# Attention and NF4 FFN on one core: wider scale loads, shifted pieces of the NF4 stream, and GpSimd taking the hidden-state splits

## The chip, the core and the metric

The kernel runs on one core of one Trainium2 chip. The core has TensorE (matmuls; the trace shows weight loads, PEld, apart from matmuls, PE), VectorE (DVE), ScalarE (ACT), GpSimd (POOL) and SyncE (SP), which issues nearly all transfers. Each engine works through its own list of instructions in order and waits on semaphores; 16 DMA engines move the data. The metric is the device time of one execution in microseconds. Before the change it was 789.08 us, the median of 3 runs (787.16 to 791.25).

## The reference

x is 8 batches of 128 rows of 512 floats, ctx the same shape. One cross-attention block with 32 query heads and 8 key/value heads of size 128, then a gated FFN whose three weights (hidden size 1376) are quantized to NF4 and back before they are used, all in float32.

```python
def nf4_quant_dequant(w):
    flat = w.reshape(-1, 64)
    absmax = jnp.max(jnp.abs(flat), axis=1, keepdims=True)
    normalized = flat / jnp.where(absmax == 0, 1.0, absmax)
    bounds = (NF4_CODE[:-1] + NF4_CODE[1:]) * 0.5
    idx = jnp.searchsorted(bounds, normalized)
    return (NF4_CODE[idx] * absmax).reshape(shape)
...
q = apply_rope(query @ Wq); k = apply_rope(key @ Wk); v = value @ Wv
logits = 30 * tanh(einsum(q, k) * 0.0883883 / 30)
weights = softmax(where(mask, logits, -1e30))
x = x + (weights @ v) @ Wo          # query is layernorm(x), key and value are ctx
h = silu(y @ dq1.T) * (y @ dq2.T)   # y is layernorm(x), dq1..dq3 went through NF4
x = x + h @ dq3.T
```

## The kernel before

**Matmuls.** Each float32 factor is split into a high and a low part (`split`, L154: ScalarE copies the high part in a rounded format, a second engine, named in the call, subtracts it from the source for the low part). `product` (L165) then makes three matmuls (high by low, high by high, low by high) for each pair of 128-row tiles, so that a 128x512 output over a depth of 512 takes 12 matmuls.

**Stages.** First the key and value projections and the first queries (0 to 124 us), written by a plan by tile number. Then 64 attention steps `i`, in 16 units `u` of four batches each: unit `u` belongs to key/value head `u // 2` and to the half `u % 2` of the batches, and step `i` to batch `bb = i % 4` of that unit. In one step TensorE makes: the query projection of head `bb` for the next unit (`pq`), the output projection of step i-3 (`po`), the transposes of step i-2 (`pt_a`), the values of step i-1 (`pv`), and the scores of step i (`pl`). After that comes the FFN's gate and up loop over 22 (half, hidden tile) pairs (`pg`, `pu`; to 724 us) and the down products (`pd`).

**The query's way.** VectorE multiplies `pq` by the cosine and sine tables into `cs_q` (L518); SP moves the two swapped halves, 64 rows each, into `full_q` (L521, L522); GpSimd adds (L525); `split` makes `qr` of it (ScalarE copy at L155, GpSimd subtraction at L156); the scores of the next unit read `qr`. In the steps with `bb == 3` the add stands ahead of the scores and the split behind them.

**The scores' way.** `pl` goes through tanh and exp on ScalarE (L815, L816), is multiplied by the mask on GpSimd (L818), and is the weights of `pv` in the next step.

**The NF4 stream.** `quantize` (a generator) works through 17 units of weights, 128 x 1024 each for most: `Up` units for w1 and w2 (ten of 256 columns and one of 2 x 128), and six `Down` units for w3. For each unit it loads the weights and the reciprocal scales, GpSimd normalises (L210), 15 bounds follow (a Relu on ScalarE at L200, an accumulation on VectorE at L204 or L206), and VectorE multiplies by the scales (`finish`). `store` splits the result. `pump(n)` runs n pieces of this stream, where a piece is about one bound, and the step's order fixes where the pieces stand among the other instructions of each engine. `Scales` units find absolute maxima between the bounds. `ask` queues the loads by rank; `serve`, twice a step, issues one of them, so that they stand on SP between the step's own loads.

**Scales.** The maxima of w1 and w2 are written to `scale_d` in DRAM and read back so that each value stands on the 64 partitions of its block (`Up.scale`, L264; `begin(1)` reads the reciprocals, `begin()` the maxima). Those of w3 go through `scale3_d`, written by eight stores (L369) and read by `Down.scale` (L226), each row repeated on 32 partitions.

**The FFN.** `load_w12` (L860) reads the finished w1/w2 tiles from DRAM, from the fourth tile on by GpSimd's own queue; each load waits until the matmuls have left one of six `wq` buffers. `split_h` (L1041) splits the hidden state into `hs`: four times in the last iterations of the gate and up loop, and then one or two for each down product.

Of the kernel before, what the change touches and what calls it, by code (L numbers as in the profile page):

```python
# [11 lines left out]
F32 = mybir.dt.float32  # L12
# [8 lines left out]
P = 128  # L21
B, T, D = 8, 128, 512
NH, NKV, HD = 32, 8, 128
G = NH // NKV
# [38 lines left out]
def block_kernel(ctx: ExitStack, tc: tile.TileContext, x, ctxt, mask, wq, wk, wv, wo, w1, w2, w3, w12t, w3_t,  # L63
# [151 lines left out]
    class Down(Unit):  # L215
# [10 lines left out]
        def scale(self, t):  # L226
            s = self.tile("nf_s", f"s{t}")
            for h in self.tiles:
                g = 1 + h * P // 32
                src = scale3_d[t, g:g + self.p // 32].rearrange("g e p -> g (e p)")  # L230
                for j in range(self.p // 32):
                    nc.sync.dma_start(self.part(s, h)[j * 32:(j + 1) * 32], src[j:j + 1].to_broadcast([32, D]))
            return s

        def load(self):
# [16 lines left out]
    class Up(Unit):  # L252
# [11 lines left out]
        def scale(self, t):  # L264
            s = self.tile("nf_s", f"s{t}")
            for j, part in self.parts(s):
                for half in range(2):
                    src = scale_d[self.start // (2 * P), t, j, half, :, :self.r]
                    nc.sync.dma_start(part[half * BLK:(half + 1) * BLK],
                                      src.unsqueeze(0).to_broadcast([BLK, KT, self.r]))  # L270
            return s

        def load(self):
# [57 lines left out]
    class Scales3:  # L331
# [23 lines left out]
        def turn(self, tag):  # L355
            pt = bank(tag, "pt_ar3").rearrange("b (t p) -> b t p", p=P)[:self.nb, :2]
            for t in range(2):
                E.transpose(pt[:, t], self.s[:, t], ident)

            def later():  # L360
                leave()
                art = nf.tile([self.nb, 2, P], F32, tag="nf_t", name="art3")
                S.copy(art, pt)
                half, stores = self.nb // 4 + 1, []
                for e in range(4):
                    first = (0, 21, 43, 64)[e]
                    g = 1 - e % 2
                    for t in range(2):
                        stores.append(lambda t=t, g=g, e=e, first=first: nc.sync.dma_start(  # L369
                            scale3_d[t, g:g + 2 * half, e].rearrange("(b g) p -> b g p", g=2),  # L370
                            art[first:first + half, t].unsqueeze(1).to_broadcast([half, 2, P])))
                for some in (stores[:4], stores[4:]):
                    ask(None, lambda some=some: [f() for f in some])
            stored.append(later)
# [95 lines left out]
    with ExitStack() as c1:  # L470
# [432 lines left out]
        for i in range(N):  # L903
            u, kv, b, bb = where(i)
            s8 = i % 8
            tiles = {0: (0, 1), 1: (2,), 2: (3,), 3: ()}.get(i, (bb,)) if u + 1 < 2 * NKV else ()

            turns = [q_proj(u + 1, g) for g in tiles]
            if i == 0:
                load_o(0, 0)  # L910
                todo["k", 0, 0]()
                adds.append(turns.pop(0)())
                load_o(0, 1)
                end_store()
                copied = ending[0]()
            if i != 2:
                adds += [f() for f in turns]
            if i == 0:
                load_o(0, 2)
                load_o(0, 3)  # L920
                ending[1]()
                copied()
            if kv + 1 < NKV:
                if s8 == 3:
                    load_kv(kv + 1)
                if 4 <= s8:
                    load_o(kv + 1, s8 - 4)
                elif kv:
                    load_q(kv + 1, s8)
                due.setdefault(max(i + 1, 2), []).append(("q" if s8 < 4 else "o", kv + 1, s8 % 4))  # L930
            if s8 == 0 and kv:
                load_key(kv, 1)
            if s8 == (0 if kv else 1):
                due.setdefault(i + 1 if kv else 3, []).append(("k", kv, 1))
            if s8 == 4 and kv + 1 < NKV:
                load_key(kv + 1, 0)
                due.setdefault(i + 1, []).append(("k", kv + 1, 0))
            if i == 1:
                V.tensor_tensor(lo, whole.pop(0)[2], hi, ALU.subtract)
            if i > 3:  # L940
                store()
                end_store()
            if i > 2:

                for _ in range(2):
                    serve()
            pump(2.3 if i == 4 else 2.15 if 4 < i < 58 else 2 if i == 58 else 0)
            if 0 <= i - 3:
                project(i - 3)
            if whole and i > 3:  # L950
                *own, full = whole.pop(0)
                split(*of_head(*own), full, Q)
            if i in (59, 61):
                ln = LayerNorm((i - 59, i - 58), f"y{i - 59}")
            if 0 <= i - 2:
                turn(i - 2)
            if i == 2:
                for _ in range(1, G):
                    todo[due[2].pop(0)]()
            if 59 <= i < 63:  # L960
                ln.sums(i - 59)
            if 0 <= i - 1:
                values(i - 1)
            if i == 2:
                adds += [f() for f in turns]
            if i == 0:
                end_store()
            if adds and i > 2 and bb == 3:
                whole.append((u + 1, bb, adds.pop(0)()))
            scores(i)  # L970
            if adds:
                whole.append((u + 1, bb, adds.pop(0)()))
            if i == 61:
                xn.update({k: pair.rows(k, "xn") for k in (0, 1)})
            if whole and i > 3 and bb == 3:
                *own, full = whole.pop(0)
                split(*of_head(*own), full, Q)
            pump(1 if 2 < i < 59 else 0)
            if i == 62:
                turned((0, 1), "qq")  # L980
            if i in (60, 62):
                ln.finish(Q)
                pair = ln
            normalize()
            leave()
            if i == 0:
                pump(1)
                hi, lo = of_head(1, 0)
                S.copy(hi, whole[0][2])
            while len(whole) > 3 - i and 1 < i < 4:  # L990
                *own, full = whole.pop(0)
                split(*of_head(*own), full, Q if i > 2 else V)
            if i == 2:
                pump(1)
            for k in due.pop(i, ()):
                todo[k]()
            if i == 1:
                load_q(1, 0)
                load_key(0, 1)
                load_q(1, 1)  # L1000
            if i == 2:
                load_q(1, 2)
                load_q(1, 3)
            if i >= 61:
                load_w12(i - 61)
# [35 lines left out]
    def split_h(b, i):  # L1041
        n = min(4, NHT - 4 * i)
        if (b, i) in last_hs:
            w = last_hs.index((b, i))
            if not last_at:
                last_at.append(wide("hs_67"))
            t = hs[b, i] = last_at[0][:, :, :, w * P:(w + 1) * P]
        else:
            t = hs[b, i] = wp.tile([P, 2, KT, P], F32R, tag="wq", name=f"hs_{b}_{i}", bufs=6)
        split(t[:, 0, :n], t[:, 1, :n], hT[b // 4, i][:, :, b % 4 * T:b % 4 * T + T], V)  # L1050

    order = [(0, 2), (1, 0), (1, 1), (1, 2)] + [(half, h) for h in range(3, NHT) for half in range(2)]
    most = [(b, i) for b in range(6) for i in range(2)]
# [5 lines left out]
    for n, (half, h) in enumerate(order):  # L1059
        evac()  # L1060
        evac = gate_up(half, h, f1)
        pump((3.6 if n < last - 3 else 2.6) if n > 0 else 0)
        store()
        if n in w12_at:
            load_w12(w12_at[n])
        if n >= last - 3:
            split_h(*to_split.pop(0))
    evac()
# [3 lines left out]
    for b, i in down:  # L1072
# [9 lines left out]
        if (b, i) in most:  # L1082
            if i == 1:
                product(pd[b], mine, stop=False)
                mine.clear()
            pump(2)
            store()
        elif i == 2:
            o = f1.tile([P, D], F32, tag="o", name=f"o_{b}", bufs=4)
            parts = 2 if b == B - 1 else 1  # L1090
            for j in range(parts):
                own = slice(j * D // parts, (j + 1) * D // parts)
                to = pd[b] if b < 6 else bank(("q", "q", "s")[b - 6 + j], f"pd_{b}_{j}")
                product(to[:, own], [(s, (th[:, own], tl[:, own])) for s, (th, tl) in mine], start=b >= 6)
                V.tensor_tensor(o[:, own], acc[b][:, own], to[:, own], ALU.add)
                nc.sync.dma_start(out[b][:, own], o[:, own])
# [36 lines left out]
```

## Time and profile before

| | us |
|---|---|
| median of 3 runs | 789.08 |
| profiled execution: its own time | 789.4 |
| profiled execution: span from first to last instruction | 787.6 |
| projections, 0 to 124: PE / DVE / ACT / POOL busy | 122.4 / 95.2 / 81.4 / 70.2 |
| attention, 124 to 568 | 436.2 / 391.4 / 340.8 / 358.2 |
| end of attention and gate/up, 568 to 724 | 153.2 / 130.6 / 102.1 / 46.2 |
| down products, 724 to 788 | 60.4 / 41.1 / 27.8 / 4.8 |

TensorE's granted clock is 1.00 of full in the first three stretches and 0.99 in the last. In the lines of a timeline the columns are: start, duration, engine, line, operation, out<-in, shapes, count of merged instructions, and in brackets the idle time just before it with what ended it. For SP the duration is that of issuing, not of the transfer; the landings stand in the semaphore records of the trace.

### The profile page before, as it was taken

What the parts mean: (1) busy time and instruction counts of PE and PEld (TensorE: products, weight loads), DVE (VectorE), ACT (ScalarE), POOL (GpSimd) and SP (SyncE); (2) the same over time, 40 slices, a digit from 0 to 9 for tenths busy, and PEclk for the clock granted to TensorE, in tenths of its full rate; (3) what the DMA queues carried; (4) which work ended last, traced back from release to release, by engine and by line L of the source; (5) the groups of instructions that cost most, each with busy time, mean ns of one, the idle gap of its engine ahead of it and who ended that gap; (6) DMA issues with size and microseconds to landing.
All of it is one profiled execution on the core that took longest, in us unless ns stands there. A gap on an engine that the chain in (4) does not pass through costs nothing.

```text
span 787.6 us, 11542 instructions
## 1 busy us (share of the span) xinstructions
PE 772.1 (98%) x3800; PEld 637.3 (81%) x3800; DVE 658.3 (84%) x863; ACT 552.1 (70%) x782; POOL 479.4 (61%) x418
## 2 busy tenths in 40 slices
PE   9999999999999999999999999999999999998998
PEld 7888887788878888888788877877888888886887
DVE  6768978979889889889789988798888697899981
ACT  7558657787886868687768868687642786779740
POOL 2569446787879789797888878887750222332100
PEclk9999999999999999999999999999999999999999
DMA  6966658637373837546473745463540334633011
GB/s 219 324 202 199 189 161 240 176 115 218 104 230 87 262 92 223 172 136 201 121 233 82 213 108 182 114 175 108 181 153 1 95 103 124 185 111 110 1 54 53
DMA packets 73219, 119.24 MB, mean 151 GB/s; under 512 B 9896, under 2 KB 31080, under 8 KB 73160
## 3 DMA queue, kind: packets, MB, share of 16 engines
q1 hardware_dynamic: 70856, 110.13, 47.0%
q0 software_dynamic: 2304, 8.39, 3.4%
q8 instruction: 30, 0.49, 0.3%
q14 instruction: 29, 0.24, 0.1%
HBM read 79.32 MB, written 22.38 MB: 129 GB/s over the span
## 4 chain that ended last, share of the span: by engine, by line
PE 65%; ACT 8%; POOL 7%; DVE 6%; DMA 6%; issue 5%; SPq 3%; POOLq 0%; DVEq 0%
PE po L170 15%; PE pq L170 13%; PE pd L170 8%; PE pvp L170 6%; ACT nm_w L200 5%; PE pv L825 5%; PE pl L170 4%; PE pk L170 3%; PE pg L170 3%; PE pu L170 3%; DVE nc_w L206 3%; DMA s_w<-scale_d 2%; PE pt_a L162 2%; PE pk L611 2%; DMA w_w<-in_w3t 2%
## 5 line engine op out<-in xcount | busy, mean ns | idle before, releaser
L206 DVE SCALAR_TENSOR_TENSOR nc_w<-nm_w,nc_w 128x1024 f32<-128x1024 bf16 (+1 forms) x238 | 284.0, 1193 | 48.9 <-ACT nm_w L200 38.6
L200 ACT ACTIVATE nm_w<-w_w,bias 128x1024 bf16<-128x1024 f32 (+1 forms) x255 | 276.2, 1116 | 45.7 <-POOL w_w L210 37.3
L170 PE MATMUL po<-wo,aT 128*128 128x512 f32 x768 | 192.7, 399 | 4.1 <-DVE acc L839 3.6
L170 PE MATMUL pq<-xT,wq 128*128 128x512 f32 x768 | 186.8, 392 | 1.9 <-DVE wq L156 1.2
L170 PEld LDWEIGHTS po<-wo,aT 128*128 128x128 f32 x768 | 141.5, 188 | 44.0 <-DVE aT L156 3.9
L170 PEld LDWEIGHTS pq<-xT,wq 128*128 128x128 f32 x768 | 143.4, 188 | 35.6 <-DVE cs_q L518 2.5
L818 POOL TENSOR_TENSOR th<-th,mt 128x512 f32<-128x512 f32 x64 | 83.6, 1306 | 60.8 <-ACT th L816 56.8
L525 POOL TENSOR_TENSOR full_q<-cs_q,full_q 128x512 f32<-128x512 f32 x64 | 83.4, 1303 | 21.0 <-DMA full_q<-cs_q 17.2
L156 POOL TENSOR_TENSOR qr<-full_q,qr 128x512 fp32r<-128x512 f32 x58 | 75.4, 1301 | 8.1 <-ACT qr L155 6.8
L518 DVE TENSOR_TENSOR cs_q<-pq,cq 128x1024 f32<-128x1024 f32 x64 | 77.6, 1214 | 0.9 <-POOL full_q L525 0.8
L825 PE MATMUL pv<-vt,th 128*128 128x129 f32 x512 | 68.2, 276 | 0.9 <-POOL th L818 0.9
L170 PE MATMUL pg<-xT,w 128*128 128x512 f32 x264 | 63.8, 391 | 2.8 <-ACT w3t L155 2.8
L815 ACT ACTIVATE th<-pl 128x512 f32<-128x512 f32 x64 | 38.3, 598 | 39.0 <-PE pl L170 38.7
L825 PEld LDWEIGHTS pv<-vt,th 128*128 128x128 f32 x512 | 62.2, 192 | 2.0 <-POOL th L818 1.7
L210 POOL TENSOR_TENSOR w_w<-w_w,s_w 128x1024 f32<-128x1024 f32 (+1 forms) x17 | 39.7, 2334 | 39.1 <-DMA s_w<-scale_d 39.0
L170 PE MATMUL pu<-xT,w 128*128 128x512 f32 x264 | 63.5, 389 | 0.0
L155 ACT CAST qr<-full_q 128x512 fp32r<-128x512 f32 x63 | 38.6, 612 | 34.0 <-POOL full_q L525 32.7
L170 PE MATMUL pl<-qr,krt 128*128 128x512 f32 x192 | 60.3, 422 | 0.9 <-POOL qr L156 0.8
L170 PE MATMUL pd<-w3t,hs 128*128 128x512 f32 (+3 forms) x297 | 60.6, 366 | 0.0
L170 PEld LDWEIGHTS pg<-xT,w 128*128 128x128 f32 x264 | 49.2, 188 | 13.3 <-ACT w3t L155 3.2
L170 PEld LDWEIGHTS pd<-w3t,hs 128*128 128x128 f32 (+1 forms) x297 | 51.4, 189 | 9.2
L170 PEld LDWEIGHTS pu<-xT,w 128*128 128x128 f32 x264 | 49.6, 188 | 10.4
(122 smaller groups left out, 1078.4 us busy)
## 6 DMA issues: line engine op xcount, KB each, us to landing
full_q<-cs_q SPq DMA_DIRECT2D x128, 128.0 KB
w12t_d<-dqt SPq DMA_DIRECT2D x22, 512.0 KB
s_w<-scale_d SPq DMA_DIRECT2D x40, 256.0 KB
raw_wq<-in_L_xattn_Wq SPq DMA_DIRECT2D x32, 256.0 KB
raw_wo<-in_L_xattn_Wo SPq DMA_DIRECT2D x32, 256.0 KB
w<-w12t_d POOLq DMA_DIRECT2D x16, 512.0 KB, 4.5
s_w<-scale_d SPq DMA_DIRECT2D x86, 64.0 KB
ws<-in_L_ffn_w SPq DMA_DIRECT2D x20, 256.0 KB
```

The costliest lines, as they stand in the source:

```text
L155: S.copy(hi, src)
L156: engine.tensor_tensor(lo, src, hi, ALU.subtract)
L162: E.transpose(pt[:, k * P:(k + 1) * P], src[:, k * P:(k + 1) * P], ident)
L170: E.matmul(out, a, b, start=start and i + j == 0, stop=stop and i == n - 1 and j == 2)
L200: S.activation(m, self.w, AF.Relu, bias=bias[:self.p, i:i + 1], scale=BIG if up else -BIG)
L206: V.scalar_tensor_tensor(self.c, m, step, self.c, ALU.min, ALU.subtract if i == POS[0] else ALU.add)
L210: Q.tensor_tensor(self.w, self.w, self.s, ALU.mult)
L518: V.tensor_tensor(cs, src.rearrange("p (b t) -> p b t", t=T).unsqueeze(1).to_broadcast([P, 2, 4, T]), table.unsqueeze(2).to_broadcast([P, ...
L525: Q.tensor_tensor(full, cs[:, 0], full, ALU.subtract)
L815: S.activation(th, pl, AF.Tanh, scale=ATTN_MULT / CAP)
L818: Q.tensor_tensor(em[i], em[i], mt.unsqueeze(1).to_broadcast([P, G, T]), ALU.mult)
L825: E.matmul(pv[:, g, :HD + 1], em[i][:, g], vt[kv][:, b], start=True, stop=True)
```

## The change

1. `Down.scale`: one load of all rows of a tile in place of one for each 32 rows. `Up.scale`: for units of 256 columns one load of 128 rows in place of two of 64; the last w1/w2 unit keeps its halves.
2. The eight stores to `scale3_d` are cut differently: each writes one of the two rows of a pair for both kinds of scales, from a source without repetition.
3. In attention, `pump(2.15)` becomes `pump(2.08)`, and 2.3 in step 4 becomes 1.3. The second `pump(1)` of a step moves ahead of the query split of the steps with `bb == 3`; in step 3 it goes to the step's end, behind the key split.
4. The first query weight of the second head group is loaded in step 0, into a buffer of the tag `aT`, in place of at the end of step 1.
5. In the gate and up loop `load_w12` comes ahead of `pump` and `store`, and the last four iterations pump 3.6 like the others, in place of 2.6. `split_h` subtracts on GpSimd, in place of VectorE. In the down products `pump(2)` becomes `pump(2.1)`.

```diff
@@ Down.scale
-                for j in range(self.p // 32):
-                    nc.sync.dma_start(self.part(s, h)[j * 32:(j + 1) * 32], src[j:j + 1].to_broadcast([32, D]))
+                n = self.p // 32
+                nc.sync.dma_start(self.part(s, h), src.unsqueeze(1).to_broadcast([n, 32, D]))
@@ Up.scale
+                own = scale_d[self.start // (2 * P), t, j, :, :, :self.r]
+                if self.r == 2 * P:
+                    nc.sync.dma_start(part, own.unsqueeze(1).to_broadcast([2, BLK, KT, self.r]))
+                    continue
                 for half in range(2):
-                    src = scale_d[self.start // (2 * P), t, j, half, :, :self.r]
                     nc.sync.dma_start(part[half * BLK:(half + 1) * BLK],
-                                      src.unsqueeze(0).to_broadcast([BLK, KT, self.r]))
+                                      own[half].unsqueeze(0).to_broadcast([BLK, KT, self.r]))
@@ Scales3.turn
-                    for t in range(2):
-                        stores.append(lambda t=t, g=g, e=e, first=first: nc.sync.dma_start(
-                            scale3_d[t, g:g + 2 * half, e].rearrange("(b g) p -> b g p", g=2),
-                            art[first:first + half, t].unsqueeze(1).to_broadcast([half, 2, P])))
+                    for i in range(2):
+                        stores.append(lambda i=i, g=g, e=e, first=first: nc.sync.dma_start(
+                            scale3_d[:, g + i:g + i + 2 * half:2, e].rearrange("t b p -> b t p"), art[first:first + half]))
@@ attention step, i == 0, behind copied()
+                early.append(at.tile([P, 2, G, T], F32, tag="aT", name="raw_wq_1")[:, 0].rearrange("p g t -> p (g t)"))
+                load_q(1, 0)
+                due[2].append(("q", 1, 0))
...
-                due.setdefault(max(i + 1, 2), []).append(("q" if s8 < 4 else "o", kv + 1, s8 % 4))
+                if i:
+                    due.setdefault(i + 1, []).append(("q" if s8 < 4 else "o", kv + 1, s8 % 4))
...
-            pump(2.3 if i == 4 else 2.15 if 4 < i < 58 else 2 if i == 58 else 0)
+            pump(1.3 if i == 4 else 2.08 if 4 < i < 58 else 2 if i == 58 else 0)
...
+            pump(1 if 3 < i < 59 else 0)
             if whole and i > 3 and bb == 3:
                 *own, full = whole.pop(0)
                 split(*of_head(*own), full, Q)
-            pump(1 if 2 < i < 59 else 0)
...
+            if i == 3:
+                pump(1)
             if i == 1:
-                load_q(1, 0)
@@ split_h
-    split(t[:, 0, :n], t[:, 1, :n], hT[b // 4, i][:, :, b % 4 * T:b % 4 * T + T], V)
+    split(t[:, 0, :n], t[:, 1, :n], hT[b // 4, i][:, :, b % 4 * T:b % 4 * T + T], Q)
@@ gate and up loop
-        pump((3.6 if n < last - 3 else 2.6) if n > 0 else 0)
-        store()
         if n in w12_at:
             load_w12(w12_at[n])
+        pump(3.6 if n > 0 else 0)
+        store()
@@ down products
-            pump(2)
+            pump(2.1)
```

## The prediction

> **What bounds it now.** I read the page's engine totals first, then TensorE's timeline by step, then the timelines of the engines that TensorE waits for. A step of the attention loop shows as one x12 group of `po` matmuls.
>
> ```profile
> PE 772.1 (98%) x3800; PEld 637.3 (81%) x3800; DVE 658.3 (84%) x863; ACT 552.1 (70%) x782; POOL 479.4 (61%) x418
> ...
> q1 hardware_dynamic: 70856, 110.13, 47.0%
> ```
> ```profile
> 458.73 2.97 PE L170 MATMUL po<-wo,aT 128*128 128x512 f32 x12
> ...
> 463.02 1.16 PE L825 MATMUL pv<-vt,th 128*128 128x129 f32 x8 [0.88 <-POOL th L818]
> ...
> 467.46 2.97 PE L170 MATMUL po<-wo,aT 128*128 128x512 f32 x12
> ...
> 475.03 2.97 PE L170 MATMUL po<-wo,aT 128*128 128x512 f32 x12
> ```
> TensorE is the bound: 98% busy. The undisturbed step is 475.03 - 467.46 = 7.57 us; the one before it took 8.73, because the values matmul waited for GpSimd. From 123.71 (first `po`) to 562.82 (57th) are 56 steps in 439.1 us; at 7.575 they would take 424.2. So 14.9 us is all that attention can give back. The FFN loop runs at its floor but for one wait of 2.80 us (a `pg` at 712.79). What made that step slow:
>
> ```profile
> 449.98 1.11 SPq L269 DMA_DIRECT2D s_w<-scale_d  x2
> 453.92 0.48 SPq L521 DMA_DIRECT2D full_q<-cs_q  x1
> 454.45 1.66 SPq L522 DMA_DIRECT2D full_q<-cs_q  x1
> ```
> ```profile
> 458.07 2.41 POOL L210 TENSOR_TENSOR w_w<-w_w,s_w 128x1024 f32<-128x1024 f32 x1 [4.30 <-DMA s_w<-scale_d]
> 460.44 1.30 POOL L156 TENSOR_TENSOR qr<-full_q,qr 128x512 fp32r<-128x512 f32 x1
> 461.70 1.27 POOL L818 TENSOR_TENSOR th<-th,mt 128x512 f32<-128x512 f32 x1
> 462.93 1.26 POOL L525 TENSOR_TENSOR full_q<-cs_q,full_q 128x512 f32<-128x512 f32 x1
> ```
> GpSimd works in order. It stood 4.30 us for a scale load, so its mask product `th` came late and TensorE stood. In undisturbed steps `th` is ready 3.1 us before `pv` starts (end of L818 to start of L825, the commonest value of 64 steps); 4.30 - 3.1 = 1.2 agrees with the step's excess of 8.73 - 7.57 = 1.16. **This is the price I use: lateness on GpSimd less 3.1 us.**
>
> **Scale loads (L264, L226).** Ten w1/w2 units of 256 columns load their scales twice, so 20 loads of 512 KB. Before: two 64-row halves each; after: one DMA whose destination counts 128 rows and whose source counts 2, with the 64-fold repeat inside. SP saves one issue (0.59 us) in each, off the path. The question is over how many DMA engines it spreads. The semaphore records show it for the old ones: an SP DMA leaves 16 ticks, whether it has 32, 64, 96 or 128 rows; the eight stores of L369 alone leave 12 (one as the issue ends, eleven with the data). Their destination counts 44 rows and their source 22, and 11 divides both; where the sides differ elsewhere (128 against 512 or 1024) both are multiples of 16. That row can't tell whether 22 or 44 decided. So bounds: 16 engines, or 2 (the source's count).
> By packet records, 4096 bytes take one engine 159 ns (median of 10,112 packets). Over 16 engines the 128 packets are 8 x 0.159 = 1.3 us on each; over 2 they are 64 x 0.159 = 10.2 us. I take 2, since L369 is the nearest row and it lost engines by its shape.
>
> The Trainium skill, "DMA: Bandwidth & Descriptors", section "Why a DMA increments its semaphore by 16 and not by 1", says that the largest number up to 16 that divides the outermost counts of both sides is used, and "Rules for kernel authors" names a leading broadcast of c copies as confined to c engines: 2 here, which L369's eleven supports and no row proves. The same rules section advises one 128-partition transfer in place of two halves, which would speak for the change; by that the sum is rival 1's 784, by the other 825.
>
> What is behind it: all SP transfers share q1, and the next `full_q` transfer has a sixteenth of its rows on each engine. It queues: behind the scale load issued at 356.8 it landed 4.7 us after its own issue, 1.7 undisturbed. Before, scale loads landed 4.8 to 7.9 us after their issue; with 8.9 more on two engines (10.2 - 1.3), 13.7 to 16.8. The next `full_q` landed 6.8 to 11.1 us after that issue and its add L525 began at 7.7 to 12.9. For each of the 17 such loads inside attention I took landing + 8.9 less the add's start: 3.2 to 6.8 us late, 90.6 in all, 5.3 on average (the load issued at 403.23 landed 6.7 after, the add began 9.0 after: 6.7 + 8.9 - 9.0 = 6.6). Less 17 x 3.1: **+38 us**. Lower bound: if GpSimd's idle time of a step (7.57 less its 358 of 444 us, 81%: 1.4 us) also absorbs, 90.6 - 17 x 4.5 = +14. Upper: all of it passes on, +91. ScalarE's copy of `qr` (L155) waits for that add too, with tanh and exp behind it; these reach `th`, the same deadline. Three loads fall into the projections: the normalise at 49.6 already waited 3.32 us; +8.9 there holds `cs_k` on GpSimd. Bounds 0 and 3 x 5.8 = 17; I take **+3**, as two `q` banks and the value tiles in between give TensorE other work.
>
> The w3 loads go from 64 KB (4 per tile) to 256 KB: source count 4 (3 for the last). Two tiles are 2 x 32 packets of 2048 bytes (84 ns each) = 5.4 us on four engines, against 8 x 0.42 us of SP issue before. FFN only:
>
> ```profile
> 706.08 2.40 POOL L210 TENSOR_TENSOR w_w<-w_w,s_w 128x1024 f32<-128x1024 f32 x1 [8.02 <-DMA s_w<-scale_d]
> 708.51 3.23 ACT L200 ACTIVATE nm_w<-w_w,bias 128x1024 bf16<-128x1024 f32 x3 [4.98 <-POOL w_w L210]
> 712.79 3.00 PE L170 MATMUL pg<-xT,w 128*128 128x512 f32 x12 [2.80 <-ACT w3t L155]
> ```
> This is the one place where that wait reaches TensorE. Bounds -2.8 and the whole 5.4; I take 0, since before, too, the scales landed some 10 us after the first issue (645.05 to 655.49).
>
> **SP's block of stores (L369)** holds `full_q` behind it:
> ```profile
> 496.73 7.46 SPq L369 DMA_DIRECT2D scale_d<-art  x8
> 504.30 0.53 SPq L521 DMA_DIRECT2D full_q<-cs_q  x1
> ```
> Still eight, without the doubling read; between 0.30 (fastest L232) and 0.80 us each. The step at 515.97 took 9.35, 1.78 over. Gain 0 to 1.8: **-1**.
>
> **NF4 pieces.** 2.15 to 2.08 in 53 steps takes 0.07 x 1.19 us = 0.08 us of VectorE from each (work 7.2 of 7.57): 0 to -4.4, **-2**. Steps 3 and 4: one piece (1.19 us) moves behind the key split and one goes; the waits there were 1.20 (DVE `wq`), 0.80 and 0.79 (DVE `acc`) us, steps of 9.25 and 9.66: 0 to -3.8, **-2**. The earlier raw load of `wq_1_0` passes on SP the key load and the next `full_q` pair (one issue, 0.5 us) and moves a transfer, not its split; it sits in an `aT` buffer, so the second `aT` copy now waits for VectorE's `wq` split, which ended at 130.48, before that copy's partner began at 131.00: 0, at most 0.5. In each fourth step one bound (1.1 us on ScalarE) goes ahead of the `qr` copy: it fills a wait for L525 (32.7 us in 24 waits in all). It may hold `qr`, GpSimd's subtract and the next `pl`; TensorE's longest wait of that kind was 0.80 us. Taken at 0; without the cover 14 x 0.8 = 11. The 4.7 pieces taken out return in the last four FFN iterations: ScalarE there needs 3.6 x 15/16 x 1.07 + 0.6 (`sg`) + 0.6 (`hs`) + 0.5 (`w3t`) = 5.3 us of 5.44.
>
> **GpSimd in the FFN.** 24 `hs` splits go from 0.91 us on VectorE to 1.30 on GpSimd, which is busy 46 of 156 us there and 5 of 64 after. They are made four products (4 x 2.7 us) ahead; cost 0; with that cover gone, 24 x 0.4 = 10. Weight loads ahead of the NF4 piece: their waits for `pg`/`pu` (two near 2 us) then hold normalise, split and ScalarE's bounds; two `pg` banks cover. 0.
>
> **Sum.** 787.6 + 38 + 3 - 1 - 2 - 2 = 823.6 span; the run itself was 789.4, so + 1.8 = 825. The shown median, 789.08, is 0.3 away.
>
> **Rivals.**
> 1. *The load spreads over 16 engines* (the destination's 128 decides): +41 falls away, 784. For: SP's old loads of 64 rows all did. Against: L369. Not slower than before; it decides if scale loads land within 8 us of issue.
> 2. *Two engines, but hidden*: each lateness stays under 4.5 us, 789 to 800; TensorE's rows would show under 14 us of new waits.
> 3. *Two engines, nothing absorbed*: +91 in place of +38, 878. For: VectorE has 0.4 us spare a step; the late transfer of 361 us was paid only at 389.96 (1.47 us on `acc`).
> 4. *ScalarE becomes the FFN's bound* on top of rival 1: the last four iterations run one bound over (4 x 1.07 us) and the wait of 2.80 comes twice, +7, 791.
>
> **Chances.** Forecast 0.63 (803 to 860), rival 1 0.15, rival 2 0.10, rival 3 0.08, rival 4 0.04. About 0.5%, 3.9 us, can be told from no change. Rival 1 gives faster 0.11 and same 0.04; same also takes 0.02 of rivals 2 and 4. The range reaches from rival 1's 784 to 866, part of the way to rival 3.
>
> **What would show it.** Right: single L269 issues with 2 data ticks, landing 13 to 17 us after issue; GpSimd waiting at L525 or L210 for some 5 us after each; TensorE waits `pv` <- `th`. Wrong: landings below 8 us; or GpSimd waits with no TensorE wait. The forecast falls if SP merges the repeat with the row count before the transfer is dealt out.

## The result, and the profile after

The changed kernel takes 884.66 us (median of 4 runs, 883.74 to 885.96) against 788.12 (786.54 to 791.25): a ratio of 1.1221, 95% interval 1.1181 to 1.126. The profiled execution took 884.68 us, its span is 882.9. Slower was forecast, and by the wide scale loads; but 825 was forecast, and the range ended at 866.

The page of the kernel after: engine totals, granted clock by slice, the queue, and the chain that ended last.

```profile
PE 801.7 (91%) x3800; PEld 655.6 (74%) x3800; DVE 641.0 (73%) x839; ACT 550.6 (62%) x782; POOL 505.8 (57%) x442
...
PEclk9989999979898998999999999999999999999999
...
q1 hardware_dynamic: 68966, 110.12, 40.6%
...
PE 34%; DMA 30%; POOL 13%; issue 10%; DVE 5%; ACT 5%; SPq 2%; POOLq 0%; DVEq 0%; ACTq 0%
```

The same 3800 matmuls are busy 29.6 us longer (772.1 before): something slows the matmuls themselves, and the second line tells what, the granted clock falls below 9 tenths in five slices. The rest of the 95.3 us of span is time in which TensorE stands still: the sum of its idle time is 77.7 us against 12.2. The queue moves the same bytes at a lower share of its engines' time, so this is no lack of bandwidth over all.

By stage, with the bounds at the first `po`, the 57th `po` and the first `pd`; "clock" is half the length, inside the stage, of the records in which the granted clock is 0.5, that is the time lost by it:

| stage | before, us | after, us | TensorE idle before / after | clock before / after |
|---|---|---|---|---|
| projections, to the first `po` | 123.7 | 137.6 | 1.6 / 9.1 | 0 / 5.1 |
| attention, to the 57th `po` | 439.1 | 518.3 | 7.8 / 64.5 | 0 / 25.6 |
| to the first `pd` | 161.0 | 161.8 | 2.8 / 0.1 | 0 / 0 |
| down products | 63.8 | 65.2 | 0.0 / 4.0 | 0.5 / 0 |

The view of waits of the kernel after; the columns are who waited for whom, the sum, how often, and the longest, in us:

```profile
ACT qr L155 <- POOL full_q L527: 95.4, 27, 9.5
POOL full_q L527 <- DMA full_q<-cs_q: 94.3, 19, 10.7
POOL w_w L210 <- DMA s_w<-scale_d: 54.5, 6, 11.4
ACT dqt L155 <- DMA w12t_d<-dqt: 30.7, 5, 8.6
PE po L170 <- DVE acc L841: 25.4, 9, 6.1
PE pv L827 <- POOL th L820: 15.5, 6, 6.7
```

Before, these were 32.7, 17.2 (11 times), 39.0, 1.3, 3.6 and 0.9 (lines move by two); the second of them reads, in the same view of the kernel before:

```profile
POOL full_q L525 <- DMA full_q<-cs_q: 17.2, 11, 5.7
```

GpSimd stands for the transfer of `full_q`, ScalarE behind it for the copy of `qr`. The wait of `dqt` for the stores to `w12t_d` shows that other transfers were held too. TensorE's waits name `acc` and `th`, two or three steps down the chain.

One such event in the timeline of the kernel after, from the scale load to the last slow matmul:

```profile
257.90 0.55 SPq L269 DMA_DIRECT2D s_w<-scale_d  x1
...
262.85 0.49 SPq L523 DMA_DIRECT2D full_q<-cs_q  x1
...
263.39 0.59 SPq L524 DMA_DIRECT2D full_q<-cs_q  x1
...
263.81 1.06 PE L827 MATMUL pv<-vt,th 128*128 128x129 f32 x8
...
275.66 1.26 POOL L527 TENSOR_TENSOR full_q<-cs_q,full_q 128x512 f32<-128x512 f32 x1 [10.66 <-DMA full_q<-cs_q]
...
276.88 1.27 POOL L820 TENSOR_TENSOR th<-th,mt 128x512 f32<-128x512 f32 x1
...
276.95 0.62 ACT L155 CAST qr<-full_q 128x512 fp32r<-128x512 f32 x1 [9.05 <-POOL full_q L527]
...
278.20 2.09 PE L827 MATMUL pv<-vt,th 128*128 128x129 f32 x8 [6.66 <-POOL th L820]
...
279.94 1.63 PE L170 MATMUL pl<-qr,krt 128*128 128x512 f32 x3
...
281.36 3.86 PE L170 MATMUL pq<-xT,wq 128*128 128x512 f32 x12
```

The load is issued once, leaves three ticks (one as the issue ends, two with the data) and lands at 271.8, 13.9 us later. The two `full_q` moves issued 5 us behind it land at 275.0 and 275.5, 12.2 and 12.1 us after their issue where most undisturbed ones take 2.2 to 2.4. Their ticks in the semaphore records show the two engines directly: of the first move's sixteen, fourteen come at 264.8 to 265.7 and the last two at 274.7 and 275.0. GpSimd stands 10.66 us; its mask product `th` is next in its queue, and `pv` waits for that: 6.66 us. So 4.0 of 10.66 us were absorbed. Then the same eight `pv` matmuls take 2.09 us instead of 1.06 (the line at 263.81), three `pl` 1.63 instead of 0.93, twelve `pq` 3.86 instead of 2.90. The windows view says why; its columns are the window, its length, busy time of PE, PEld, DVE, ACT, POOL, then granted clock, DMA share and GB/s:

```profile
262.00:271.60 9.60, 9.54 (x50) 7.78 (x48) 7.47 (x9) 4.50 (x7) 2.80 (x3) 1.00 0.46 135
271.60:276.60 5.00, 0.00 (x0) 0.00 (x0) 0.00 (x0) 0.00 (x0) 0.94 (x1) 1.00 0.39 139
276.60:283.40 6.80, 5.20 (x16) 4.53 (x17) 4.09 (x6) 5.46 (x8) 4.48 (x5) 0.50 0.61 164
```

For 5 us hardly an engine works, and for the next 6.8 the clock is 0.50. This second price, 1.03 + 0.70 + 0.96 = 2.7 us here, stands in no row of the kernel before.

TensorE's longest wait has another source, GpSimd's normalise, which reads the scales themselves. The timeline of the kernel after at 188 us:

```profile
187.94 2.34 POOL L210 TENSOR_TENSOR w_w<-w_w,s_w 128x1024 f32<-128x1024 f32 x1 [10.83 <-DMA s_w<-scale_d]
190.31 1.15 ACT L200 ACTIVATE nm_w<-w_w,bias 128x1024 bf16<-128x1024 f32 x1 [14.28 <-POOL w_w L210]
193.00 0.40 PE L325 MATMUL pt_ar<-ident,ar 128*32 128x128 f32 x1 [9.52 <-ACT th L817]
193.36 5.18 PE L170 MATMUL po<-wo,aT 128*128 128x512 f32 x12
```

ScalarE works in order too: its first bound of the new unit waits for the normalise, and tanh and exp of the scores stand behind that bound. Twelve `po` matmuls take 5.18 us here, 2.97 elsewhere.

### The profile page after: what moved, and what is told of

It is laid out like the page before. It is cut to its first block, busy times and chain, and to the rows that moved or that the text cites. A ratio compares the mean times of both kernels' runs of the same rounds, so it can differ in the third digit from the quotient of the medians.

```text
span 882.9 us, 11442 instructions
## 1 busy us (share of the span) xinstructions
PE 801.7 (91%) x3800; PEld 655.6 (74%) x3800; DVE 641.0 (73%) x839; ACT 550.6 (62%) x782; POOL 505.8 (57%) x442
## 4 chain that ended last, share of the span: by engine, by line
PE 34%; DMA 30%; POOL 13%; issue 10%; DVE 5%; ACT 5%; SPq 2%; POOLq 0%; DVEq 0%; ACTq 0%
DMA full_q<-cs_q 12%; DMA w12t_d<-dqt 8%; DMA s_w<-scale_d 7%; PE po L170 7%; PE pd L170 6%; PE pq L170 5%; PE pvp L170 3%; POOL qr L156 2%; PE pv L827 2%; PE pu L170 2%; PE pg L170 2%; ACT nm_w L200 2%; DMA ws<-in_L_ffn_w 2%; DVE nc_w L206 2%; PE pl L170 2%
## 5 line engine op out<-in xcount | busy, mean ns | idle before, releaser
L170 PE MATMUL po<-wo,aT 128*128 128x512 f32 x768 | 207.0, 421 | 35.1 <-DVE acc L841 25.4
L170 PEld LDWEIGHTS po<-wo,aT 128*128 128x128 f32 x768 | 150.9, 201 | 80.2 <-ACT th L818 26.8
L170 PE MATMUL pq<-xT,wq 128*128 128x512 f32 x768 | 189.1, 395 | 1.8 <-DVE wq L156 1.3
L170 PEld LDWEIGHTS pq<-xT,wq 128*128 128x128 f32 x768 | 145.7, 190 | 35.6 <-DVE wq L156 1.7
L527 POOL TENSOR_TENSOR full_q<-cs_q,full_q 128x512 f32<-128x512 f32 x64 | 83.1, 1298 | 102.7 <-DMA full_q<-cs_q 94.3
L827 PE MATMUL pv<-vt,th 128*128 128x129 f32 x512 | 70.6, 282 | 15.5 <-POOL th L820 15.5
L520 DVE TENSOR_TENSOR cs_q<-pq,cq 128x1024 f32<-128x1024 f32 x64 | 77.7, 1215 | 2.8 <-POOL full_q L527 1.4
L210 POOL TENSOR_TENSOR w_w<-w_w,s_w 128x1024 f32<-128x1024 f32 (+1 forms) x17 | 39.5, 2324 | 60.6 <-DMA s_w<-scale_d 54.5
L170 PE MATMUL pg<-xT,w 128*128 128x512 f32 x264 | 63.8, 391 | 0.0
```

Of the source, the lines that this page charges most:

```text
L170: E.matmul(out, a, b, start=start and i + j == 0, stop=stop and i == n - 1 and j == 2)
L210: Q.tensor_tensor(self.w, self.w, self.s, ALU.mult)
L520: V.tensor_tensor(cs, src.rearrange("p (b t) -> p b t", t=T).unsqueeze(1).to_broadcast([P, 2, 4, T]), table.unsqueeze(2).to_broadcast([P, ...
L527: Q.tensor_tensor(full, cs[:, 0], full, ALU.subtract)
L827: E.matmul(pv[:, g, :HD + 1], em[i][:, g], vt[kv][:, b], start=True, stop=True)
```

## The experiments

Each experiment has its own runs of the kernel before, on the same chip; their medians lie between 788.1 and 792.6, so ratios are given. Times of different experiments are compared only roughly. "Attention" is the stage of the table above, in the profiled execution.

### Which edit it is

**e1: the changed kernel, the w1/w2 scale loads in halves again.**
```diff
-                if self.r == 2 * P:
-                    nc.sync.dma_start(part, own.unsqueeze(1).to_broadcast([2, BLK, KT, self.r]))
-                    continue
                 for half in range(2):
```


> The kernel after, with the w1/w2 scale loads back in two halves of 64 rows; all else as after. Theory Q (the wide loads run on two DMA engines, and the query moves queue behind them): nearly the whole +96 us goes, 779 to 790 us; each of these loads leaves 16 ticks again and lands within 8 us; TensorE idles under 15 us, and its granted clock stays full until the end. Rival O (the other edits - pieces moved, weight loads first, splits on GpSimd - carry a good part): above 810 us. Rival D (the wide w3 loads on four engines carry a part): 792 to 810 us.

784.88 us (782.72 to 787.09), ratio 0.9901 [0.9871, 0.993]. Attention 432.9 us, TensorE idle 9.0 in all. Twenty DMAs carry the whole loss.

**e2: all scale loads as before, the other edits kept** (in addition to e1, `Down.scale` gets its loop over 32 rows back).

> The kernel after, with both kinds of scale loads narrow as before; only the moves of pieces, stores, weight loads and splits are left. Theory Q: 779 to 790 us, within 3 us of the run with only the w1/w2 loads narrow. Rival D: at least 5 us faster than that run. Rival O: above 810 us.

780.25 us (779.65 to 782.03), ratio 0.9851 [0.9813, 0.9888]: the fastest kernel of this study, and faster than both. From the page of e2:

```profile
PE 768.3 (99%) x3800; PEld 638.7 (82%) x3800; DVE 642.1 (83%) x839; ACT 553.6 (71%) x782; POOL 507.3 (65%) x442
...
PEclk9999999999999999999999999999999999999999
```

TensorE is 99% busy and its clock whole. The wide w3 loads cost the difference to e1, 4.6 us, in this company; that lies between theory Q's 3 and rival D's 5.

**e3: the kernel before, only the w1/w2 loads wide** (the `Up.scale` part of the change alone).

> The kernel before, with only the w1/w2 scale loads made wide (one of 128 rows in place of two of 64). Theory Q: 870 to 895 us by itself, 20 loads with 2 data ticks landing 13 to 17 us after issue, TensorE idle 50 to 80 us more and some 10 or more drops of the granted clock. Rival O: under 800 us.

912.83 us (909.38 to 918.75), ratio 1.1528 [1.1467, 1.1589], more than the whole change and above theory Q's 870 to 895. Attention 546.3, idle there 85.5, clock 42.7.

### The queue, or the engines

**e4: the wide loads issued by ScalarE instead of SP.**
```diff
-                    nc.sync.dma_start(part, own.unsqueeze(1).to_broadcast([2, BLK, KT, self.r]))
+                    nc.scalar.dma_start(part, own.unsqueeze(1).to_broadcast([2, BLK, KT, self.r]))
```


> The kernel after, with the wide w1/w2 scale loads issued from ScalarE's queue in place of SP's; the same bytes on the same two engines' worth of work, but not ahead of the query moves in SP's queue. Theory Q (order within SP's queue is what costs): full_q lands 2 to 4 us after its issue, and 785 to 815 us remain. Rival E (the two engines are simply full, or the normalise waits for its own scales; the queue does not matter): 860 to 890 us.

867.59 us (864.21 to 868.14), ratio 1.0937 [1.0884, 1.099]. This was my own theory's miss: with the loads out of `full_q`'s issue queue most of the loss should have gone, and only 17 us did (22 by the ratios); rival E's 860 to 890 holds. The waits of e4:

```profile
ACT qr L155 <- POOL full_q L527: 84.4, 30, 7.4
POOL full_q L527 <- DMA full_q<-cs_q: 72.0, 26, 6.9
```

There are more waits than in the kernel after, and they are shorter. The landings say the same: `full_q` moves issued while a wide load was under way took 6.6 us (median), against 9.3 from the shared queue and 3.3 in e1. The loads themselves took longer, 13.6 to 18.5 us up to 420 us. In the packet records behind the load issued at 194.76 two packets of 4096 bytes from its queue and two of 2048 from SP's come in turn for most of the time from 202.3 to 205 us. So the two transfers now alternate, on the same two engines: order in the queue is a part of the hold (9.3 against 6.6 us), the full engines are the rest. The Trainium skill, "DMA: Bandwidth & Descriptors", section "Issuing engines are not separate DMA queues", says that DMAs of different issuers run on the same 16 engines and interleave, which the 6.6 and 9.3 us agree with.

The time of e4 overstates what is left, though, since ScalarE now has to wait for the store of the scales before it can issue their load:

```profile
263.89 0.49 ACTq L269 DMA_DIRECT2D s_w<-scale_d  x1
264.43 1.15 ACT L200 ACTIVATE nm_w<-w_w,bias 128x1024 bf16<-128x1024 f32 x1 [9.57 <-DMA scale_d<-art]
268.91 5.46 PE L170 MATMUL po<-wo,aT 128*128 128x512 f32 x12 [6.79 <-DVE acc L841]
```

With the 10.2 us of half clock from 264.1 on, this one place costs some 12 us (6.8 + 5.1) that the loads on SP do not have.

**e5: the scale rows stored eight times**, so that one load of the same 128 x 1024 values has an outermost count of 16.
```diff
-    scale_d = dram.tile([(NHT + 1) // 2, 2, 2, 2, KT, 2 * P], F32, name="scale_d")
+    scale_d = dram.tile([(NHT + 1) // 2, 2, 2, 2, 8, KT, 2 * P], F32, name="scale_d")
...
-                    nc.sync.dma_start(part, own.unsqueeze(1).to_broadcast([2, BLK, KT, self.r]))
+                    nc.sync.dma_start(part, own.rearrange("f c k h -> (f c) k h").unsqueeze(1).to_broadcast([16, BLK // 8, KT, self.r]))
...
-                nc.sync.dma_start(own.rearrange("t j f k h -> (t j f) k h"), t)
+                for k in range(KT):
+                    nc.sync.dma_start(own[:, :, :, :, k].rearrange("t j f c h -> (t j f) c h"),
+                                      t[k::KT].unsqueeze(1).to_broadcast([8, 8, P]))
```


> The changed kernel, with each pair of scale rows stored eight times, so that the single wide load of 128 partitions has an outermost count of 16 instead of 2; the same 128x1024 f32 in one DMA. The 22 stores of scale_d become 88. Theory Q2 (the cost lies in the two engines that carry a load with two outermost rows, not in there being one load): 16 + 1 ticks or 16, a landing 4 to 8 us after issue, attention from the first to the 57th output projection 431 to 440 us as with the halves (432.9), 780 to 795 us, the upper end for the added stores. Rival W (one load of 128 partitions from a broadcast source is slow as such, through its size or its place in the queue): landing over 11 us, 860 to 890.

790.76 us (787.8 to 794.79), ratio 0.9994 [0.9968, 1.002]. Sixteen ticks; the loads up to 420 us landed 4.7 to 7.5 us after issue; attention 433.4 us, as with the halves. One load instead of two does no such harm; the outermost count of 2 did. Against e1 the ratio is some 0.9% higher: the span is 4.3 us longer, 2.6 of them ahead of the first `po`, where 12 of its 44 stores of `scale_d` stand (11 in all before; the 22 and 88 of the expectation are counted wrong, and so are the 44 of e6, which has 22). The rest was not followed.

**e6: the rows stored twice**, for an outermost count of 4 (`[4, BLK // 2, KT, self.r]`, and the store made twice).

> The changed kernel, with the scale rows stored twice, so that the wide load has an outermost count of 4; 44 stores of scale_d in place of 22. By the two-engine landings of 13.2 to 15.8 us the transfer takes about 12.5 us, half of it here, so a landing 7 to 9 us after issue; the full_q moves are issued 4.5 to 7.5 us after the load and wait some 1 to 3.5 us instead of 6 to 10. Theory C (as the prediction had it: GpSimd's lateness is worth nothing up to 3.1 us a time): 783 to 792, no gaps of 2 us on TensorE. Theory D (there is no such cushion, lateness comes through at about 0.7 to 1 for 1): 20 loads by 1 to 2.5 us, 800 to 825, though with few clock drops, as the gaps are short.

816.92 us (812.98 to 821.64), ratio 1.0316 [1.0263, 1.0369]; attention 457.7. Five ticks; landings up to 420 us 8.7 to 12.4 us, later than the 7 to 9 I had expected. From the waits of e6:

```profile
POOL full_q L528 <- DMA full_q<-cs_q: 41.7, 14, 6.6
```

The time lies in theory D's 800 to 825, but it does not decide between the theories: both stood on waits of 1 to 3.5 us, and these run to 6.6. Taken one by one the waits speak for a cushion: in attention what exceeds 3.1 us in each of them, at L528 and at L210, adds up to 16.3 us (0.6 in e1), and TensorE stands 17.4 us longer there than in e1. Two, four and sixteen engines make 884.7, 816.9 and 790.8.

### From lateness to time

**e7: the kernel before, only the ten loads of the maxima wide** (`if self.r == 2 * P and t == 0`).

> The kernel before with only the 10 loads of the maxima wide (two outermost rows), those of the reciprocals left in halves; with all 20 it took 912.8 (+121). Theory L (each wide load costs its own hold, whatever the others do): half, +55 to +65, so 845 to 857. Theory A (what is late is made up between the loads, as they are twice as far apart): less than a third, +15 to +40, 805 to 830. Theory B (a wide load costs more by itself, since the second of a pair falls where the first has already made things late): over +70, 860 to 880.

841.65 us (839.14 to 844.07), ratio 1.0625 [1.0584, 1.0666]: +50, against +121 for all twenty. That lies between theory L's 845 and theory A's 830, much nearer L: most of each load's price is its own, and a little is made up when they are rarer.

The kernels together, each in attention; "over 3.1" is what exceeds 3.1 us in each of GpSimd's waits for `full_q` and, at L210, for the scales:

| kernel | GpSimd waits for `full_q`, us | over 3.1 | attention | idle | clock |
|---|---|---|---|---|---|
| before | 7.6 | 1.2 | 439.1 | 7.8 | 0 |
| e7 | 60.5 | 30.3 | 486.9 | 39.2 | 20.5 |
| e3 | 103.4 | 73.2 | 546.3 | 85.5 | 42.7 |
| e1 | 6.9 | 0.6 | 432.9 | 4.2 | 1.7 |
| e6 | 38.8 | 16.3 | 457.7 | 21.6 | 6.8 |
| e4 | 68.6 | 12.3 | 498.1 | 44.5 | 25.6 |
| after | 90.7 | 54.0 | 518.3 | 64.5 | 25.6 |

Against before (for e7, e3) or e1 (for the others) each further us of GpSimd's wait for `full_q` brought 0.55 to 0.81 us of idle TensorE (e7: 31.4 over 52.9; e3: 77.7 over 95.9), and each us of idle 0.29 to 0.65 us of clock. With the cushion taken off wait by wait, the further idle time is 1.08 to 1.13 times what is left, but for e4: its 24 shorter waits leave 11.7 us and bring 40.3. ScalarE's stand of above accounts for only 6.8 of these; why the rest came through there is open.

### The other edits

**e8: the kernel before, only the w3 scale loads wide** (the `Down.scale` part alone).

> The kernel before with only the scale loads of w3 wide (one load per tile on 4 outermost rows in place of four). Theory H (hold on the engines as with the Up loads, only shorter and in the FFN's end of the stream): the two kernels with and without it differed by 784.9 to 780.3, so +2 to +7 us here too. Rival Z (the prediction's term: FFN 0, between -2.8 and +5.4, because GpSimd there has time to spare): within 2 us of the kernel before.

804.57 us (803.16 to 806.29), ratio 1.0171 [1.0137, 1.0204]: +12, above both theories. To the first `pd` it is 167.5 us against 161.0 (idle 6.0 against 2.8, clock 3.4), and two of attention's last steps, where the stream's w3 units begin, take 4.5 and 2.8 us over the undisturbed 7.57 (1.1 and 0.1 before). GpSimd has time to spare there, but ScalarE stands longer behind its normalise (47.5 us, 37.3 before).

**e9: the kernel before, only the attention edits** (parts 3 and 4 of the change).

> The kernel before with only the attention edits (pieces of the NF4 stream ahead of the query split in each fourth step, the budgets 1.3 and 2.08, the first wq load and its steps early), all scale loads in halves. Prediction's terms: pieces -2, early steps -2, the reordering 0, so -4. Theory T (read from the stages of the changed kernel without wide loads: attention 430.6 us against 439.1): -7 to -10 us, attention 429 to 433 us. Rival N (that gain came from GpSimd's load in the FFN or the store edit, not from the order): within 2 us.

787.75 us (785.21 to 790.42), ratio 0.9956 [0.9932, 0.9981]: -5, less than theory T's -7 to -10. But attention takes 430.3 us and the next stage 157.9, 8.8 and 3.1 less than before, and the down products 71.3, 7.5 more. TensorE's timeline of e9 shows where it is given back:

```profile
724.82 21.47 PE L170 MATMUL pd<-w3t,hs 128*128 128x512 f32 x94
751.85 8.53 PE L170 MATMUL pd<-w3t,hs 96*128 96x512 f32 x29 [5.55 <-POOL w3t L156]
```

The pieces taken out of attention are done at the end, and the last w3 tile is 5.55 us late, followed by a clock record of 0.5 for 6.8 us.

**e10: the kernel before, only the FFN edits** (part 5).

> The kernel before with only the FFN edits (hs split on GpSimd in place of VectorE, the weight loads ahead of the pieces, 3.6 and 2.1 of budget). Prediction's term: 0 for both. Theory T (from the same stages, last output projection to first down projection 157.9 us against 161.0): -2 to -4 us. Rival S (GpSimd's split is slower and holds the down projections): +1 to +5 us.

793.08 us (791.05 to 797.03), ratio 1.0022 [0.9999, 1.0045]: nothing alone. With the attention edits (e2) the down products take 63.8 us again. So these edits are probably what lets the attention edits keep their gain. Which one of them (the 3.6 pieces in the last four iterations, the loads' place, or `hs` on GpSimd) was not tried; nor was the new cut of the stores (part 2), which e2 has too and e9 has not.

### Why the parts don't add up

Wide w1/w2 loads +121, wide w3 loads +12, attention edits -5, FFN edits 0 would make some 917 from 789. The whole change takes 884.7.

**e11: e3 with all attention edits**, and **e12: e3 with their order alone**:
```diff
+            pump(1 if 3 < i < 59 else 0)
             if whole and i > 3 and bb == 3:
                 *own, full = whole.pop(0)
                 split(*of_head(*own), full, Q)
-            pump(1 if 2 < i < 59 else 0)
...
+            if i == 3:
+                pump(1)
```


> The kernel before with the wide loads of w1/w2 and all attention edits; the w3 loads and the FFN as before. With the wide Up loads alone it took 912.8, and the whole change 884.7, though the attention edits alone were worth only -5 and the wide w3 loads alone +12. Theory I (the attention edits take back more where full_q comes late, because the engines have pieces to do that they would otherwise find behind the wait): 875 to 890. Theory S (they give the same -5 here as alone, and the rest comes from the FFN or the store edit): 904 to 912.

> The kernel before with the wide loads of w1/w2 and of the attention edits only the order: the piece ahead of the query split in each fourth step, and at the end of step 3. Budgets and the wq load as before. If theory I holds through the order (one bound of 1.1 us on ScalarE and 1.2 on VectorE in each fourth step goes ahead of the copy that waits for full_q): 880 to 895, most of what the attention edits give together. If through the budgets (pieces that end earlier in each step): 905 to 915.

e11: 890.79 us (886.8 to 891.74), ratio 1.1284 [1.124, 1.1329]. e12: 896.46 us (893.23 to 898.98), ratio 1.137 [1.1327, 1.1412]; both a little above theory I's ranges and far from the other theories'. Attention goes from 546.3 (e3) to 533.5 with the order and 522.1 with all; without wide loads the same edits were worth 8.8 us there, with them 24.2. My reading is that where `full_q` comes late, a piece that stands ahead of the copy which waits for it is work done, and one behind it is one more thing that is late. The idle time agrees (85.5, 70.4, 61.5 us), the clock's part less so (42.7, 44.4, 37.5); GpSimd's waits for `full_q` fall as well (103.4, 90.5, 88.5). Over 3.1 there are 57.2 us in e12 and 44.8 in e11, for 62.7 and 58.6 us more idle than in before and e9, with the loads in halves, so in e11 the cushion explains less. From e11 to the whole change the down products fall once more, from 72.9 to 65.2 us.

## Why the prediction was right, and where it failed

- **Two engines for a source of two rows:** right, with three ticks and landings 13.2 to 15.8 us after issue (13.7 to 16.8 forecast). The row of L369 was the right neighbour. Rival 1 falls with the three ticks; e5, with sixteen rows outermost, comes within a per cent of its 784. The Trainium skill ("DMA: Bandwidth & Descriptors", "Rules for kernel authors") has an outermost count below 16 confine a DMA to at most that many engines, which agrees with 884.7, 816.9 and 790.8 us for outermost counts of 2, 4 and 16; the same section's advice to use one 128-partition transfer holds here only where its source has enough rows.
- **"All SP transfers share q1 ... it queues":** `full_q` was late by the forecast amount (90.6 us in 17 events forecast; 90.7 in 16 waits of attention measured, 7.6 before), but e4 shows that the shared queue is only part of the reason: with a queue of their own the loads still leave 68.6 us there.
- **"Lateness on GpSimd less 3.1 us", +38: the step that failed.** Attention grew by 79.2 us, and by 85.4 over e1, which has the other edits: 60.3 of idle TensorE and 23.9 of clock. The first thing wrong was that the clock had no term, though TensorE was to stand for several us at a time. The second was the size of the idle time. The events were forecast at 3.2 to 6.8 us each; the waits at L527 in attention ran from 0.2 to 10.7, so that nearly the same sum leaves 45.7 us over 3.1 each, not 38. GpSimd's waits for the scales themselves at L210 were summed only in the projections; in attention they leave 8.3 more, and the one at 188 us alone made TensorE stand 9.52. And ScalarE waits in order: its copies and bounds behind the late tile delay `th`, `aT` and `acc`, so TensorE's largest wait is for `acc` (25.4 us), not for `th` alone as foretold. The cushion as such was there: 10.66 became 6.66 in the event shown, and 54.0 us over 3.1 stand beside the 60.3 of idle.
- **Rival 3, nothing absorbed, 878,** was the nearest number, by luck: 0.72 of the further lateness became idle time, and the clock added 0.29. Rival 2, lateness hidden, falls with the new idle time.
- **Projections +3:** +13.9, idle +7.5 and clock +5.1. The normalise waited 11.38 us (until 58.57) where it had waited 3.32; `pvp` then stood 4.24 us and ran twelve matmuls in 5.49. The bound of 17 held; 2.7 of the 13.9 stay in e1, without the wide loads.
- **w3 loads 0, FFN only:** 4.6 us with the other edits, 12 without; in e8 7.9 of it is in attention, which the forecast left out.
- **Stores -1, pieces -2, early steps -2, FFN edits 0:** together -1.5% (e2), about -12 us. The steps of attention give 8.5 of it. The reordering taken at 0 works together with the budgets, and the FFN edits taken at 0 are worth up to 7.5 us as part of the set, nothing by themselves; the stores were not measured alone. Rival 4, ScalarE as the FFN's bound, is not seen: 157.9 us there in e2.

## What to carry to other kernels

Before several transfers are merged into one, look at the outermost count of both sides: a repeat inside with two rows outside puts all bytes on two engines, and every transfer that needs all sixteen waits for those two, here from its own queue and from another (e4). When a wait reaches TensorE, price it one event at a time, and add what the clock takes after it. Measure the parts of a change in company, too: one set of edits here saved 5 us alone, 12 with its partners, and 19 or more where something else was late.

## What the runs showed of the hardware

**TensorE's clock falls after short waits.** In the 14 profiled executions (both kernels and e1 to e12) there are 91 stretches of clock 0.5 before the end of the span, 3.4 us long or a multiple of it, up to 13.7. Each began 1.9 to 5.3 us after the start of a TensorE wait of at least 0.8 us. Counted from the waits (without the one at the span's start):

| wait of TensorE, us | clock 0.5 begins in it or within 4 us of its end |
|---|---|
| 0.8 to 1.5 | 2 of 44 |
| 1.5 to 2 | 7 of 22 |
| 2 to 3 | 23 of 36 |
| 3 to 4 | 13 of 14 |
| 4 and more | 48 of 48 |

The Trainium skill, "TensorE: Matmul & The Clock Gate", section on the HAM clock gate (Part 1), has half rate after an idle window of about 3.4 us whose phase is the hardware's own. The traces agree on the window: in each execution all changes of the clock lie on one grid of 3.41 us, at another phase from execution to execution. But a fully idle one isn't needed, by 32 waits under 3 us that were followed by a drop. Laid on this grid, every window at full clock in which TensorE stood for more than 1.92 us was followed by half clock (84 of 84), none under 1.60 us was, and 7 of the 22 between. So about half a window is enough, and what a wait of 2 to 3 us costs depends on how the grid falls across it. Half clock ended after each window with at most 0.51 us of idle (91) and after none with 0.64 or more (55).

**Two engines shared by two queues** served `full_q` in 6.6 us (median) beside a wide load, where one queue took 9.3 and free engines 2.3.
